# Context attentions of a Perceiver block: the third group's partial sums are joined on Pool during the last group, and the last group's weights are summed into three parts instead of six

## The chip, the cores and the metric

The kernel runs on one core of a Trainium2 chip. The core has a matrix engine (TensorE, PE in the profile, with its weight loads shown apart as PEld), three engines for elementwise work (VectorE, DVE; ScalarE, ACT; GpSimd, POOL), and SyncE (SP), whose queue issues most of the DMA transfers. Each engine works through its own list of instructions in order and waits at semaphores for the others. The metric is the device time of one execution in microseconds. Three executions of the kernel before took 1450.78, 1451.24 and 1454.07 us, median 1451.24.

## The reference: what is computed

Two layers are applied to x (512 tokens of width 512). Each has an attention to a context of 8192 rows, a self attention and a feed-forward part with 8 experts, two per token. The change touches the two context attentions alone. Cut to what matters, the first one is

```python
q = _ln(q, qn_w, qn_b) * scale
k = _ln(k, kn_w, kn_b)
attn = jnp.einsum('bihd,bjhd->bhij', q, k)
attn = jnp.where(padding_mask[:, None, None, :], attn, -jnp.inf)
p = jax.nn.softmax(attn, axis=-1)
ctx = jnp.einsum('bhij,bjhd->bihd', p, v).reshape(b, s1, c)
out = ctx @ Wo.T + bo
```

The second one has no norm of q and k and masks with -1e9 instead of -inf. Each has 16 heads of 32 columns. Of the context only the rows behind a drawn length are unmasked, at most a quarter of the 8192. The kernel looks up which tiles of 128 context rows hold unmasked rows and attends to 15 tiles (SLOTS); for more there is a second, general path, which does not run on these inputs. A softmax row is p divided by its sum, so the kernel computes unnormalised weights exp(score - max), their product with v, and their sum apart, and divides at the end.

## The kernel before, in words

Both attentions run through attend_slots (line 885). The 16 heads are taken in four groups of four (NG = 4, GH = 4), and each group passes over the 15 tiles of context rows. The main loop (line 1057) therefore has 60 steps, at = 0 to 59, with g = at // 15 the group and i = at % 15 the tile.

**One step.** PE makes four score blocks, one for each head, each 128 context rows by 512 queries, in PSUM (score, line 904, its matmul at line 905), subtracts the row maxima with a bf16 matmul (subtract, L766), and ACT takes the exponential of each block into pT, a tile of 128 x 2048 fp32 in SBUF (exp, L1055). The four heads use a quarter of the array's rows each and run side by side. accumulate (L996) multiplies pT with the values (L1010, "acc") one or two steps later. While maxima of later groups are still to be found, the steps also make a second set of scores ("scm") from which DVE takes the maxima (L934). That part is done 19 steps before the end, so the last steps have scores, shift, exponentials and acc only. Groups 0 to 2 gather acc in SBUF by DVE additions (L1018); the last group gathers it in PSUM.

**The denominators.** The sum of the weights is made by a matmul of each pT with a block of ones (denominators, L1032 to L1045, matmul at L1038, "den"). To make fewer of these, add_up (L1020) first sums up to four consecutive pT into one tile "four" (L1029). Groups 0 to 2 are summed on Pool into five parts (tiles 0 to 3, 4 to 7, 8 to 11, 12 and 13, and 14 alone). The last group is summed on DVE into six (0 to 3, 4 to 7, 8 to 11, and 12, 13 and 14 alone). For each part PE makes four matmuls, one for each head.

**The order around the change.** Work that belongs to a group already passed is put into the list fillers, and at most one entry is taken after each step. For the third group (g = 2) the entries are its denominators three steps after its end, divide one step later (ACT: Ln and Exp of d, L1044 and L1049; Pool: o x d, L1050, and + bias, L1052), and its two outputs (L855, "ops", which DVE adds into x, L861) 13 and 14 steps after its end, which is after steps i=12 and i=13 of the last group. The last group's denominators stand after its steps i=13 and i=14 and around the last two accumulations. Then finish_part (L821) makes the inverse of den, the product and the bias for one half of the queries after the other (L202, L203, L816, L819), and outputs multiplies with Wo.

**Buffers.** The scores, den and ops tiles of the last group go in turn through seven PSUM banks (tags s and m, k.tags). Tile number t in this order waits until tile t - 7 has been read: score tiles by ACT, ops tiles by DVE's addition into x. In SBUF there are five buffers for pT, five for four, one for d and two for o.

**Queues.** A scheduler of the framework orders each engine's instructions when the program is built. SP's queue at the end of the first attention loads, in this order, wva, wv, wq, two halves of wide, wo, two more of wide and a bias row; then a register load from irow (values_load in ctx_slots, L734) and the context slots (cslot, L745). wva is the value weight of the second context attention, the others belong to the self attention that comes next.

Of the kernel before, what the change touches and what calls it, by code (L numbers as in the profile page):

```python
# [11 lines left out]
F32 = mybir.dt.float32  # L12
# [5 lines left out]
ALU = mybir.AluOpType  # L18
# [3 lines left out]
P = 128  # L22
S = 512
# [6 lines left out]
NG = 4  # L30
# [35 lines left out]
def tile_perceiver(  # L66
# [5 lines left out]
    nc = tc.nc  # L72
# [127 lines left out]
    def inverse(to, src):  # L200

        nc.scalar.activation(to, src, AF.Ln)  # L202
        nc.scalar.activation(to, to, AF.Exp, scale=-1.0)  # L203
# [547 lines left out]
    def in_quads(pool, psum, pacc, qT, wo, bv, late, splits=None):  # L751
# [59 lines left out]
        def begin(g):  # L811
            k.sums[g] = [pacc.tile([P, S], F32, name=name, tag=name) for name in ("acc", "den")]

        def divided(g, r, d, acc, den):
            inverse(d[:, r], den)
            nc.vector.tensor_tensor(k.o[g][:, r], acc, d[:, r], ALU.mult)  # L816
            if bv is not None:

                nc.scalar.activation(k.o[g][:, r], k.o[g][:, r], AF.Identity, bias=bv[:, g : g + 1])  # L819

        def finish_part(g, r, acc, den):  # L821

            if g not in k.o:
                k.o[g] = late().tile([P, S], F32, name="o", tag="o", bufs=2)
            divided(g, r, late().tile([P, S], F32, name="d", tag="d", bufs=1), acc, den)

        def finish(g, pieces=1):

# [31 lines left out]
                else:  # L860
                    nc.vector.tensor_tensor(x[:, t, :], x[:, t, :], ps, ALU.add)  # L861

        k.tile_s, k.subtract, k.shift_of = tile_s, subtract, shift_of
        k.begin, k.finish, k.finish_part, k.outputs, k.quotient = begin, finish, finish_part, outputs, quotient
        return k

# [18 lines left out]
    def attend_slots(pool, psum, pacc, kT, vN, qT, kbias, krow, wo, bv, late, keys, settle, values, unit, more, early, aside, beside, extra, plan, tail, phase=None):  # L885
# [133 lines left out]

        def add_up(g, i, pT):  # L1020

            engine = nc.gpsimd if g < NG - 1 else nc.vector
            if i % 4 == 0 or i >= (n - 1 if g < NG - 1 else (n - 1) // 4 * 4):
                parts[g].append(pT)
                return
            to = parts[g][-1]
            if i % 4 == 1:
                to = late().tile([P, GH, S], F32, name="four", tag="four", bufs=5)
            engine.tensor_tensor(to, parts[g][-1], pT, ALU.add)  # L1029
            parts[g][-1] = to  # L1030

        def denominators(g, which, end):  # L1032

# [13 lines left out]
        def divide(g):  # L1047

            nc.scalar.activation(dens[g], dens[g], AF.Exp, scale=-1.0)  # L1049
            nc.gpsimd.tensor_tensor(k.o[g], k.o[g], dens[g], ALU.mult)  # L1050

            nc.gpsimd.tensor_scalar(k.o[g], k.o[g], bv[:, g : g + 1], None, ALU.add)  # L1052
# [4 lines left out]
        for at in range(NG * n):  # L1057
# [23 lines left out]
            else:  # L1081
# [6 lines left out]
                    exp(pT, h, i, tiles[h])  # L1088
                accumulate(2)
            add_up(g, i, pT)  # L1090
            if i == n - 1 and g < NG - 1:
                fillers.extend((
                    (at + 3, lambda g=g: denominators(g, range(len(parts[g])), len(parts[g]))),
                    (at + 4, lambda g=g: divide(g)),
                    (at + (13 if g == NG - 2 else 10), lambda g=g: k.outputs(g, (0, 1))),
                    (at + (14 if g == NG - 2 else 11), lambda g=g: k.outputs(g, (2, 3))),
                ))
            behind.append((g, i, pT))
            fillers.sort(key=lambda f: f[0])
            if fillers and fillers[0][0] <= at:  # L1100
                fillers.pop(0)[1]()
            if g == NG - 1 and i >= n - 2:

                lone = n - (n - 1) // 4 * 4
                whole = (n - 1) // 4
                end = whole + lone
                denominators(g, range(0, whole - 1) if i == n - 2 else range(whole - 1, end - 2), end)
        accumulate(1)
        denominators(NG - 1, range(end - 2, end), end)
        accumulate(1)  # L1110
        for _, f in fillers:
            f()
        for i in range(2):
            r = slice(i * S // 2, (i + 1) * S // 2)
            k.finish_part(NG - 1, r, k.sums[NG - 1][:, r], dens[NG - 1][:, r])
        k.outputs(NG - 1, range(NT))

    def columns(pool, vector, tag):
# [1542 lines left out]
```

## Time and profile before

| | us |
|---|---|
| median of three executions | 1451.24 |
| the profiled execution | 1449.59 |
| its span | 1447.9 |
| PE busy in it | 1408.3 |
| DVE busy | 701.3 |
| ACT busy | 582.3 |
| POOL busy | 426.7 |

The last group of the first attention runs from 345 to 394 us of the span, that of the second from 1111 to 1159 us. In lists of groups an entry is: line, engine, operation, tile written <- tiles read, shape, count, and then durations in nanoseconds as least/median/most. In timelines an entry starts with its start and its length in microseconds, and ends in brackets with the idle time before it and what ended that. In the chain of work that ended last an entry has its start, its length, the engine and the tile. fp32 matmuls have two records each, and matmuls of four heads run side by side, so 40 den records are 20 matmuls, or five parts.

### The profile page before, as it was taken

What the parts mean: (1) busy time and instruction counts of PE and PEld (TensorE: products, weight loads), DVE (VectorE), ACT (ScalarE), POOL (GpSimd) and SP (SyncE); (2) the same over time, 40 slices, a digit from 0 to 9 for tenths busy, and PEclk for the clock granted to TensorE, in tenths of its full rate; (3) what the DMA queues carried; (4) which work ended last, traced back from release to release, by engine and by line L of the source; (5) the groups of instructions that cost most, each with busy time, mean ns of one, the idle gap of its engine ahead of it and who ended that gap; (6) DMA issues with size and microseconds to landing.
All of it is one profiled execution on the core that took longest, in us unless ns stands there. A gap on an engine that the chain in (4) does not pass through costs nothing.

```text
span 1447.9 us, 25019 instructions
## 1 busy us (share of the span) xinstructions
PE 1408.3 (97%) x9827; PEld 866.4 (60%) x9827; DVE 701.3 (48%) x1987; ACT 582.3 (40%) x1168; POOL 426.7 (29%) x359
## 2 busy tenths in 40 slices
PE   8989999999999999999999999999999999999997
PEld 3434444443244558899999766644444235499993
DVE  5458598985523525111111226768986525741112
ACT  2656466677723252111111121166667822411221
POOL 2151078987011110200001110058987010111002
PEclk9999999999999999999999999999999999999999
DMA  8455200000040004987889450000000050059575
GB/s 247 152 190 148 71 31 1 2 1 1 26 185 1 15 23 164 389 304 269 270 279 302 152 178 24 30 1 2 1 1 2 1 189 1 16 207 338 192 247 183
DMA packets 94267, 175.15 MB, mean 121 GB/s; under 512 B 5496, under 2 KB 32182, under 8 KB 92348
## 3 DMA queue, kind: packets, MB, share of 16 engines
q1 hardware_dynamic: 87004, 151.43, 30.9%
q0 software_dynamic: 6416, 19.94, 3.8%
q10 hardware_dynamic: 720, 2.10, 0.4%
q8 instruction: 79, 1.29, 0.4%
q14 instruction: 48, 0.39, 0.1%
HBM read 162.72 MB, written 9.68 MB: 119 GB/s over the span
## 4 chain that ended last, share of the span: by engine, by line
PE 84%; DMA 3%; DVE 2%; ACT 1%; issue 1%; SPq 1%; POOL 0%; POOLq 0%; ACTq 0%; DVEq 0%
PE hps L2226 12%; PE y L2247 11%; PE sc L905 11%; PE acc L1010 8%; PE prj L1573 4%; PE pk L1387 4%; PE scm L923 4%; PE ops L855 3%; PE den L1038 3%; PE sc L923 3%; PE pv L1199 2%; PE sc L766 2%; DMA w<-in_L_ffn_W 2%; PE pva L1514 2%; PE pk L1199 1%; PE pv L1423 1%
## 5 line engine op out<-in xcount | busy, mean ns | idle before, releaser
L1055 ACT ACTIVATE pT<-sc,kbias 128x512 f32<-128x512 f32 x480 | 288.6, 711 | 95.6 <-PE sc L766 85.5
L934 DVE CUSTOM_DVE_ANT_0 masked<-scm,krowb 128x512 f32<-128x512 f32 (+2 forms) x400 | 213.9, 591 | 39.7 <-PE scm L923 38.1
L905 PE MATMUL sc<-qTf,kTf 32*128 32x512 f32 x960 | 216.7, 621 | 1.5 <-DVE tops L934 1.5
L2226 PE MATMUL hps<-tokens,w 128*128 128x160 f32 (+11 forms) x1408 | 194.3, 294 | 3.5 <-DMA w<-in_L_ffn_W 3.5
L2226 PEld LDWEIGHTS hps<-tokens,w 128*128 128x128 f32 x1408 | 185.5, 192 | 6.5 <-issue 3.8
L923 PE MATMUL scm<-kTf,qTf 32*128 32x512 f32 (+2 forms) x800 | 189.0, 539 | 0.0
L2247 PE MATMUL y<-hT,w 128*128 128x160 f32 (+11 forms) x1280 | 177.2, 297 | 1.1 <-DMA w<-in_L_ffn_W 1.1
L2247 PEld LDWEIGHTS y<-hT,w 128*128 128x128 f32 x1280 | 170.1, 192 | 3.6 <-DVE hT L2480 1.1
L1029 POOL TENSOR_TENSOR four<-four,pT 128x2048 f32<-128x2048 f32 x36 | 164.0, 4555 | 1.6
L905 PEld LDWEIGHTS sc<-qTf,kTf 32*128 32x128 f32 x960 | 73.7, 183 | 95.6 <-DVE tops L934 42.5
L1010 PE MATMUL acc<-pT,vNf 128*32 128x512 f32 x960 | 127.8, 604 | 0.0
L1029 POOL TENSOR_TENSOR four<-pT 128x2048 f32<-128x2048 f32 x24 | 109.3, 4556 | 54.0 <-ACT pT L1055 54.0
L934 DVE CUSTOM_DVE_ANT_0 masked<-sc,krowb 128x512 f32<-128x512 f32 (+2 forms) x176 | 98.5, 614 | 54.9 <-PE sc L923 54.5
L2475 DVE TENSOR_TENSOR hT<-sg,hps 128x264 f32<-128x264 f32 (+7 forms) x64 | 28.0, 437 | 194.5 <-ACT sg L2474 187.6
L2474 ACT ACTIVATE sg<-hps 128x264 f32<-128x264 f32 (+7 forms) x64 | 25.4, 397 | 180.1 <-PE hps L2226 175.3
L923 PEld LDWEIGHTS scm<-kTf,qTf 32*128 32x128 f32 x800 | 86.1, 184 | 15.3 <-issue 6.2
L766 PE MATMUL sc<-shift,ones 3*128 3x512 bf16 (+3 forms) x544 | 93.4, 367 | 0.0
L2278 POOL DMA_DIRECT2D answers_d<-yb x17 | 9.6, 566 | 243.4 <-ACT yb L2265 243.2
L1018 DVE TENSOR_TENSOR o<-o,acc 128x512 f32<-128x512 f32 x84 | 57.4, 683 | 20.5 <-PE acc L1010 20.5
L1010 PEld LDWEIGHTS acc<-pT,vNf 128*32 128x32 f32 x960 | 19.3, 108 | 70.3 <-DVE tops L934 34.7
L1199 PE MATMUL pv<-wkvf,cslot 128*128 128x512 f32 x120 | 54.9, 606 | 1.8 <-DVE tops L934 1.1
L1656 DVE TENSOR_REDUCE neg<-sc 128x1 f32<-128x512 f32 (+3 forms) x64 | 26.9, 484 | 60.0 <-PE sc L1652 60.0
(394 smaller groups left out, 1874.0 us busy)
## 6 DMA issues: line engine op xcount, KB each, us to landing
w<-in_L_ffn_W SPq DMA_DIRECT2D x94, 1024.0 KB, 5.4
mi<-in_mask SPq DMA_DIRECT2D x32, 512.0 KB, 4.6
cslot<-in_ctxT SPq DMA_DIRECT2D x40, 256.0 KB, 3.9
answers_d<-yb POOLq DMA_DIRECT2D x13, 256.0 KB, 4.0
answers_d<-zero POOLq DMA_DIRECT2D x9, 256.0 KB, 3.0
wkvf<-in_L_xattn_WkvT SPq DMA_DIRECT2D x8, 256.0 KB, 6.9
wof<-in_L_xattn_WoT SPq DMA_DIRECT2D x2, 1024.0 KB
wide<-in_L_attn_wk SPq DMA_DIRECT2D x4, 512.0 KB
```

The costliest lines, as they stand in the source:

```text
L766: nc.tensor.matmul(ps, lhsT=ones16[r, :], rhs=k.shifts[g][r, 0:w], start=start, stop=stop)
L905: nc.tensor.matmul(ps, lhsT=kT[HD * h : HD * (h + 1), g, i * P : (i + 1) * P], rhs=qT[HD * h : HD * (h + 1), g, :], start=True, stop=stop,)
L923: nc.tensor.matmul(ps[:, at : at + w], lhsT=qT[HD * h : HD * (h + 1), g, t * P : (t + 1) * P], rhs=kT[HD * h : HD * (h + 1), g, lo : lo + ...
L934: nc.vector.tensor_tensor_reduce(masked[:, 0:w], ps[:, at : at + w], krow[:, lo : lo + w], 1.0, -BIG, ALU.add, ALU.max, accum_out=tops[g % ...
L1010: nc.tensor.matmul(acc[HD * h : HD * (h + 1), :], lhsT=vN[:, i, g * P + HD * h : g * P + HD * (h + 1)], rhs=pT[:, h, :], start=alone or i ...
L1029: engine.tensor_tensor(to, parts[g][-1], pT, ALU.add)
L1055: nc.scalar.activation(pT[:, h, :], ps, AF.Exp, bias=kbias[:, i : i + 1])
L1199: last = nc.tensor.matmul(ps.rearrange("p (g n) -> p g n", g=NG), lhsT=src[:, c, s % 2, :], rhs=wkv[:, :, c, i * P : (i + 1) * P], start=( ...
L1387: end = nc.tensor.matmul(ps[:, j], lhsT=wk[:, g, c], rhs=src[:, c], start=(c == 0), stop=(c == NC - 1))
L1573: nc.tensor.matmul(ps, lhsT=w(c), rhs=xnT[:, c, off : off + S], start=(c == 0), stop=(c == NC - 1))
L2226: end = nc.tensor.matmul(ps[:, j, 0:k], lhsT=w1[:, c, f * P : (f + 1) * P], rhs=tokens[:, c, starts[r] : starts[r] + k], start=(c == 0), s ...
L2247: nc.tensor.matmul(accs[0][:, d, 0:k], lhsT=w2[:, f, d * P : (d + 1) * P], rhs=hT[:, f, 0:k], start=(c == 0 and f == 0 and d % 2 == 0), st ...
```

## The change

For the third group, three additions are put on Pool after step i=14 (fewer): the part of tile 14 into that of tiles 12 and 13, and the parts of tiles 0 to 3 and 4 to 7 into that of tiles 8 to 11. Two parts stay instead of five. Its denominators come eight steps after the group's end instead of three, divide nine instead of four; the outputs stay where they were.

For the last group, tile 12 is added to the part of tiles 8 to 11 on DVE; the part of tiles 0 to 3 is added to that of 4 to 7 on Pool at step i=8, and the result to that of 8 to 11 on DVE at step i=11. Three parts stay instead of six: tiles 0 to 12, 13 and 14. Their matmuls stand after the loop, with no den matmuls after steps i=13 and i=14.

At the end, the inverses of both halves are made before both products, in one tile d for both.

In the built program the order of PE, DVE, ACT and POOL differs from before in these places only. On DVE the new join and the addition of tile 12 stand ahead of the four additions of the third group's ops into x. On ACT the last Ln, Ln, Exp, Exp, + bias, + bias replace Ln, Exp, + bias twice. On SP the register load from irow and the first cslot load now stand between wva and wv at the end of the first attention; the second attention's order on SP is as before.

```diff
--- before.py
+++ after.py
@@ -811,9 +811,8 @@
         def begin(g):
             k.sums[g] = [pacc.tile([P, S], F32, name=name, tag=name) for name in ("acc", "den")]
 
-        def divided(g, r, d, acc, den):
-            inverse(d[:, r], den)
-            nc.vector.tensor_tensor(k.o[g][:, r], acc, d[:, r], ALU.mult)
+        def divided(g, r, d, acc):
+            nc.vector.tensor_tensor(k.o[g][:, r], acc, d, ALU.mult)
             if bv is not None:
 
                 nc.scalar.activation(k.o[g][:, r], k.o[g][:, r], AF.Identity, bias=bv[:, g : g + 1])
@@ -822,7 +821,9 @@
 
             if g not in k.o:
                 k.o[g] = late().tile([P, S], F32, name="o", tag="o", bufs=2)
-            divided(g, r, late().tile([P, S], F32, name="d", tag="d", bufs=1), acc, den)
+            d = late().tile([P, S], F32, name="d", tag="d", bufs=1)
+            inverse(d[:, r], den)
+            divided(g, r, d[:, r], acc)
 
         def finish(g, pieces=1):
 
@@ -860,7 +861,7 @@
                 else:
                     nc.vector.tensor_tensor(x[:, t, :], x[:, t, :], ps, ALU.add)
 
-        k.tile_s, k.subtract, k.shift_of = tile_s, subtract, shift_of
+        k.tile_s, k.subtract, k.shift_of, k.divided = tile_s, subtract, shift_of, divided
         k.begin, k.finish, k.finish_part, k.outputs, k.quotient = begin, finish, finish_part, outputs, quotient
         return k
 
@@ -1019,15 +1020,28 @@
 
         def add_up(g, i, pT):
 
-            engine = nc.gpsimd if g < NG - 1 else nc.vector
-            if i % 4 == 0 or i >= (n - 1 if g < NG - 1 else (n - 1) // 4 * 4):
+            final = g == NG - 1
+            if i % 4 == 0 and not (final and i >= n - 3) or i >= n - (2 if final else 1):
                 parts[g].append(pT)
                 return
             to = parts[g][-1]
             if i % 4 == 1:
                 to = late().tile([P, GH, S], F32, name="four", tag="four", bufs=5)
-            engine.tensor_tensor(to, parts[g][-1], pT, ALU.add)
+            (nc.vector if final else nc.gpsimd).tensor_tensor(to, parts[g][-1], pT, ALU.add)
             parts[g][-1] = to
+            if final and i == n - 4:
+                join(g, 1, 0, nc.vector)
+
+        def join(g, to, of, engine):
+
+            pin(engine.tensor_tensor(parts[g][to], parts[g][to], parts[g][of], ALU.add))
+            parts[g].pop(of)
+
+        def fewer(g):
+
+            join(g, 3, 4, nc.gpsimd)
+            join(g, 1, 0, nc.gpsimd)
+            join(g, 1, 0, nc.gpsimd)
 
         def denominators(g, which, end):
 
@@ -1088,10 +1102,13 @@
                     exp(pT, h, i, tiles[h])
                 accumulate(2)
             add_up(g, i, pT)
+            if i == n - 1 and g == NG - 2:
+                fewer(g)
             if i == n - 1 and g < NG - 1:
+                rest = 8 if g == NG - 2 else 3
                 fillers.extend((
-                    (at + 3, lambda g=g: denominators(g, range(len(parts[g])), len(parts[g]))),
-                    (at + 4, lambda g=g: divide(g)),
+                    (at + rest, lambda g=g: denominators(g, range(len(parts[g])), len(parts[g]))),
+                    (at + rest + 1, lambda g=g: divide(g)),
                     (at + (13 if g == NG - 2 else 10), lambda g=g: k.outputs(g, (0, 1))),
                     (at + (14 if g == NG - 2 else 11), lambda g=g: k.outputs(g, (2, 3))),
                 ))
@@ -1099,20 +1116,22 @@
             fillers.sort(key=lambda f: f[0])
             if fillers and fillers[0][0] <= at:
                 fillers.pop(0)[1]()
-            if g == NG - 1 and i >= n - 2:
-
-                lone = n - (n - 1) // 4 * 4
-                whole = (n - 1) // 4
-                end = whole + lone
-                denominators(g, range(0, whole - 1) if i == n - 2 else range(whole - 1, end - 2), end)
+            if g == NG - 1 and i == n // 2 + 1:
+                join(g, 1, 0, nc.gpsimd)
+        end = len(parts[NG - 1])
+        denominators(NG - 1, (0,), end)
         accumulate(1)
-        denominators(NG - 1, range(end - 2, end), end)
+        denominators(NG - 1, range(1, end), end)
         accumulate(1)
         for _, f in fillers:
             f()
+        r = slice(0, S // 2), slice(S // 2, S)
+        d = late().tile([P, S], F32, name="d", tag="d", bufs=1)
+        k.o[NG - 1] = late().tile([P, S], F32, name="o", tag="o", bufs=2)
         for i in range(2):
-            r = slice(i * S // 2, (i + 1) * S // 2)
-            k.finish_part(NG - 1, r, k.sums[NG - 1][:, r], dens[NG - 1][:, r])
+            inverse(d[:, r[i]], dens[NG - 1][:, r[i]])
+        for i in range(2):
+            k.divided(NG - 1, r[i], d[:, r[i]], k.sums[NG - 1][:, r[i]])
         k.outputs(NG - 1, range(NT))
 
     def columns(pool, vector, tag):
```

## The prediction

> **What bounds the kernel now.** I read the page first. TensorE (PE) is busy for 97% of the span, so the change can pay only by taking work off PE, and only where PE does not then wait for the engine that took the work over.
>
> ```profile
> PE 1408.3 (97%) x9827; PEld 866.4 (60%) x9827; DVE 701.3 (48%) x1987; ACT 582.3 (40%) x1168; POOL 426.7 (29%) x359
> ```
>
> Next the chain of work that ended last, in the last group of the first attention (335 to 400 us):
>
> ```profile
> 351.80 4.29 PE den L1038 x40
> 356.09 1.07 PE sc L905 x8
> 357.17 0.22 PE sc L766 x4
> 357.38 0.99 PE acc L1010 x8
> ...
> 378.99 1.91 PE ops L855 x4
> ...
> 383.19 1.91 PE ops L855 x4
> 385.10 1.85 PE den L1038 x16
> ...
> 389.24 1.72 PE den L1038 x16
> ...
> 391.81 1.84 PE den L1038 x16
> ...
> 394.89 6.80 DMA wv<-in_L_attn_wv
> ```
>
> It is PE without a break. One step (scores, shift, acc) is 1.07 + 0.22 + 0.99 = 2.28 us; 40 den records, that is five parts, are 4.29, so a part is 0.86 us. ACT needs 0.58 for each of a step's four exponentials, 2.33 us, hardly more than PE's step.
>
> Last the adds that the change gives to Pool and DVE, by line 1029 and by the timelines of both engines:
>
> ```profile
> L1029 POOL TENSOR_TENSOR four<-four,pT x36: 4536/4554/4572, 191.8 to 1105.9; 128x2048 f32<-128x2048 f32 x36
> L1029 DVE TENSOR_TENSOR four<-four,pT x12: 2291/2293/2294, 353.6 to 1144.3; 128x2048 f32<-128x2048 f32 x12
> ```
> ```profile
> 344.78 4.56 POOL L1029 TENSOR_TENSOR four<-pT 128x2048 f32<-128x2048 f32 x1
> ```
> ```profile
> 351.16 2.29 DVE L1029 TENSOR_TENSOR four<-pT 128x2048 f32<-128x2048 f32 x1 [0.88 <-ACT pT L1055]
> ```
>
> In this kernel Pool's last add ends (349.34) before DVE's first begins (351.16): the two never add side by side. After the change they do. What happens then shows elsewhere: a 64x15 DVE instruction that ends with a Pool add, and small and large Pool instructions that begin while DVE reads two SBUF operands.
>
> ```profile
> 205.59 4.55 POOL L1029 TENSOR_TENSOR four<-four,pT 128x2048 f32<-128x2048 f32 x1
> ```
> ```profile
> 207.78 2.38 DVE L694 TENSOR_SCALAR taken<-steps,place,some 64x15 f32<-64x15 f32 x1
> ```
> ```profile
> L694 DVE TENSOR_SCALAR taken<-steps,place,some x2: 285/1334/2383, 6.3 to 207.8; 64x15 f32<-64x15 f32 x2
> ```
> ```profile
> 120.24 0.69 DVE L1354 TENSOR_TENSOR kb<-kb,un_v 128x512 f32<-128x512 f32 x1
> ```
> ```profile
> L1464 POOL TENSOR_SCALAR first<-mi x32: 207/218/762, 34.2 to 172.0; 128x2 f32<-128x2 int32 x32
> ```
>
> The 64x15 instruction takes 0.285 us alone and 2.383 here: it ends at 210.16, the Pool add at 210.14. In the other direction a Pool instruction of 0.218 us, begun at 120.25, takes 0.762 and ends at 121.01, just after the DVE add at 120.93. So each engine waits for the other's whole instruction, up to a handover: Pool lets go about 0.285 - 0.02 = 0.26 us before its end, DVE about 0.218 - 0.08 = 0.14.
>
> **The change, part by part.** Per attention (there are two):
>
> Off PE: the third group's den has two parts for five, the last group's three for six; 6 x 0.86 = 5.1 us off the path.
>
> Onto Pool: three joins of 4.55 us behind its last add of the third group, and one more at step i=8 of the last group. In Pool's queue o x d and + bias (1.28 and 1.57 us) stand behind the first three, the fourth behind these. Onto DVE: one join and the add of i=12, 2.29 us each; behind them in its queue stand the four adds into x that empty the PSUM banks of ops. On PE the moved den waits for the third join, on ACT the two activations on d wait for that den, and the exponentials of i=8 on stand behind them.
>
> Without any contest for the port I replayed the last group, each engine in its order, each instruction at its row's duration when engine and inputs are ready, 0.1 us for a semaphore. The same replay of before ends at 394.39, the trace's last acc at 394.35. Pool's joins run from 349.37 to 363.11. PE, no longer held by den at 351.80, comes to den after five steps at 363.24, just behind them. DVE then does i=11 to 378.1, the join to 380.5, i=12 from 380.6 to 382.9, and only then the first add into x, to 383.7. PE wants the bank that this empties at 381.5, for the second ops of i=13, and gets it at 383.8: 2.3 us lost. The last acc ends at 391.34, so 3.05 us earlier per attention.
>
> With the port as those rows show it, the two alternate. Join 1: 349.37 to 353.92. DVE's add of i=1, ready at 351.08, gets the port at 353.66 and ends at 355.96; join 2 355.82 to 360.37; add 2 to 362.41; join 3 362.27 to 366.82. PE's den starts at 366.92 for 363.24: 3.7 us lost. DVE goes on late: add 3 to 368.85, add 5 to 371.25, then behind o x d add 6 to 374.42, behind + bias add 7 to 377.88, add 9 to 380.28. The fourth join takes 380.14 to 384.69; adds 10 and 11 end at 389.12, the join on DVE at 391.51, i=12 at 393.90, the first add into x at 394.69. PE would have made that second ops at 385.22 and makes it at 394.79: 9.6 us lost. The last acc ends at 402.33 for 394.39, 7.9 us later; so -5.1 + 3.7 + 9.6, and some small change.
>
> The unknown price is the handover. Held to the very end of each instruction, the replay gives +10.2 us; let go by Pool 0.9 before its end and by DVE 0.14, +4.1; if Pool keeps the port from join 1 into join 2 (no wait stands between them), +8.5. I take +7.9, by the two rows, and keep +3.5 to +10.4.
>
> The Trainium skill (SBUF — State Buffer, section SBUF: two separate sides) states that a DVE instruction with two SBUF inputs and a Pool instruction that reads SBUF lock each other out for the full instruction, which speaks against this change. By the rule alone it would be +10.2. One row differs from it: a DVE add that starts at 359.86 while Pool's + bias lasts from 358.88 to 360.45, and neither is longer than elsewhere; so the rows' handover goes before the rule.
>
> The tail. Both Ln now stand before the first Exp on ACT, so the first half of o comes one Ln (0.38 us) later, and ops, norm and the next stage with it: +0.4. The second half comes earlier, hidden under the two ops of the first half (1.9 us). On SP the first attention's order changes: a register load from irow and one cslot load (256 KB) come between wva and wv. The register load's rows are 1.4 to 1.6 us and the issue 0.4, so wv is issued 2 us later. That lies under wva's own transfer (1 MB, some 2.4 us at the 430 GB/s of that stretch); cslot's 256 KB take 0.6 us in front of wv. PE waits for wv there already (1.5 us), so between 0 and 2.6 us; I take +0.7, which covers the 0.4 of this attention too. The second attention's SP order is the same.
>
> At nothing: the freed buffers. The weights of i=14 are freed by join 1 (353.92), before the exponentials of i=4 want them (355.6); the sums' buffers by joins 2 and 3, before adds 5 and 9. If Pool came 2 us later still, these would wait first.
>
> Sum: 2 x 7.9 + 0.7 + 0.4 = +16.9 us. The profiled execution took 1449.59 us (span 1447.9), so 1466.5; it lies 1.65 under the median 1451.24, and for the median I say 1468.
>
> **The rivals.** First, no contest between the two adds (the faster side). For it: the row at 359.86, with 0.59 us of overlap and no delay. Against: the 2.1 us wait at 207.78, though of an instruction of another kind. It gives 2 x -3.05 + 1.1 = -5.0, 1446. The point from which it decides: DVE's i=12 ends at 382.9 there, and every us that this comes later moves the end by about as much; one block of 2.5 us per attention eats it.
>
> Second, only Pool waits: DVE takes the port at once. For it: Pool's 0.762 at 120.25, and a Pool add of 4.93 us at 72.60 beside 4.52 elsewhere. Against: 207.78 again. Joins then end at 364.9, den waits 1.8 us, the fourth join ends at 375.6; -1.4 per attention, with the tail -1.7: 1449.5, no change.
>
> Third, Pool keeps the port over all its joins. For it: Pool's adds follow each other within 0.05 us. Against: the 64x15 instruction did get in between two Pool adds. It gives +9.0 per attention: 1470.
>
> **How the numbers follow.** Alternation, with the third rival as its upper end, 85%; only Pool waits 8%; no contest 7%. A measurement of this kernel tells about 0.3%, 4.4 us, from no change: no contest at -5.0 stands at the edge and gives faster 6% and same 1%; only Pool waits is same; alternation at +3.5 to +10.4 per attention, +8 to +22, is all slower. The likeliest one's own range is 1459 to 1474. The range leaves out the two rivals below, and reaches a little past the handovers on both sides: 1456 to 1476.
>
> **What would show it.** In the changed profile: DVE's adds of line 1029's group longer than 2.29 us, or starting well after their exponentials, beside Pool's joins, up to 4 us each; PE's den of the third group waiting some 3 to 4 us for Pool; PE's second ops of i=13 waiting some 9 us for DVE's add into x; the last group, 49.4 us from its first scores (344.95) to its last acc, about 57. Den records 240 where there were 336. The prediction is wrong if DVE's adds stay at 2.29 us and follow their exponentials at once: then the port is not contested. It is wrong in size if PE's two waits are there but the joins end well before 366.

## The result, and the profile after

The changed kernel took 1472.43 us, the median of four executions (1469.55 to 1473.89); the kernel before took 1451.01 beside it (1449.29 to 1454.07). The ratio is 1.0143, with a 95% interval from 1.0119 to 1.0166: 21.4 us slower. The forecast was 1468 with a range of 1456 to 1476. The profiled execution took 1473.18 us, its span 1471.5 (before: 1447.9).

First the page's line of busy time:

```profile
PE 1410.4 (96%) x9731; PEld 863.8 (59%) x9731; DVE 745.6 (51%) x1991; ACT 581.5 (40%) x1168; POOL 480.9 (33%) x367
```

PE has 96 records fewer, the den that the change took off it, and is nevertheless busy for 2.1 us more: some of its instructions must have become longer. The chain of work that ended last, in the last group of the first attention, is no longer PE without a break (start, length, what):

```profile
349.64 11.07 POOL four L1037 x2
...
360.79 6.46 POOL four L1037
...
367.29 3.69 PE den L1052 x16
...
372.34 2.79 POOL o L1064
...
375.21 3.48 POOL o L1066
378.69 5.95 POOL four L1037
...
405.56 1.39 SPq L734
...
407.59 5.84 DMA wv<-in_L_attn_wv
```

Pool's joins (L1037) stand where PE's scores and accumulations stood; the second and third take 6.5 us each instead of the 4.5 of such an add. The same stretch on DVE, as a timeline (start, length, line; in brackets the idle time before):

```profile
351.40 4.92 DVE L1030 TENSOR_TENSOR four<-pT 128x2048 f32<-128x2048 f32 x1 [0.88 <-ACT pT L1069]
356.42 12.96 DVE L1030 TENSOR_TENSOR four<-four,pT 128x2048 f32<-128x2048 f32 x2
...
380.35 8.84 DVE L1030 TENSOR_TENSOR four<-four,pT 128x2048 f32<-128x2048 f32 x2
389.29 2.29 DVE L1037 TENSOR_TENSOR four<-four 128x2048 f32<-128x2048 f32 x1
391.69 2.29 DVE L1030 TENSOR_TENSOR four<-four,pT 128x2048 f32<-128x2048 f32 x1
393.89 1.88 DVE L862 TENSOR_TENSOR x<-x,ops 128x512 f32<-128x512 f32 x3
```

The first three adds take 4.92 and 12.96 us where three times 2.29 would do, as long as Pool's joins last; two more take 8.84 beside the fourth join. The first add into x can only begin at 393.89. And on PE:

```profile
367.29 3.64 PE L1052 MATMUL den<-four,ones 128*32 128x512 f32 x16 [3.31 <-POOL four L1037]
370.86 2.03 PE L906 MATMUL sc<-qTf,kTf 32*128 32x512 f32 x8
...
394.63 2.08 PE L856 MATMUL ops<-wof,o 128*128 128x512 f32 x2 [6.14 <-DVE x L862]
396.64 2.09 PE L906 MATMUL sc<-qTf,kTf 32*128 32x512 f32 x8
```

These are the two waits that were forecast: 3.3 us for Pool's third join and 6.1 us for DVE's first add into x. Not forecast is what follows each of them: 16 den records take 3.64 us, eight score records 2.03 and 2.09. In the same view of before they take 1.92 and 1.14:

```profile
385.03 1.92 PE L1038 MATMUL den<-four,ones 128*32 128x512 f32 x16
386.88 1.14 PE L905 MATMUL sc<-qTf,kTf 32*128 32x512 f32 x8
```

The windows of the profile after say why (stretch, its length, busy time and count of the five engines, then PE's granted clock):

```profile
366.00:372.60 6.60, 5.31 (x24) 1.28 (x28) 6.50 (x3) 1.23 (x2) 1.50 (x2) 0.50 0.00 0
372.90:393.00 20.10, 15.60 (x118) 4.04 (x114) 18.89 (x7) 14.08 (x24) 11.64 (x3) 1.00 0.00 1
393.40:399.80 6.40, 5.17 (x18) 1.39 (x22) 3.06 (x5) 0.57 (x1) 0.00 (x0) 0.50 0.00 0
400.10:405.00 4.90, 4.90 (x49) 1.28 (x39) 0.00 (x0) 2.32 (x6) 0.02 (x1) 1.00 0.01 2
```

PE's clock is at half for some 6.5 us around the end of each wait. In before it is whole all through the last group.

Two lengths, read from the PE timelines, carry the comparison from here on: the last group (from its first scores to the end of its last acc) and the tail (from there to the first projection of the next stage, vps). Attention 1 / 2, in us:

| profile | last group | tail |
|---|---|---|
| before, three executions | 49.5 / 49.5 each | 7.4 to 7.6 / 9.0 |
| after | 59.7 / 58.3 | 8.7 / 9.6 |
| after, once more | 58.2 / 60.2 | 8.7 / 9.1 |
| third group's part alone | 53.7 / 52.6 | 7.6 / 9.4 |
| last group's part and new end | 53.2 / 54.4 | 8.5 / 9.1 |
| the same with Pool memsets | 54.3 / 55.7 | 8.4 / 9.1 |
| new end alone | 49.5 / 49.5 | 8.5 / 9.6 |
| PE kept at work in its waits | 56.8 / 56.9 | 8.8 / 9.2 |
| adds into x first on DVE | 54.5 / 54.0 | 8.9 / 9.1 |
| all joins on DVE, two executions | 46.4 / 46.4 each | 7.5, 7.6 / 9.0 |

### The profile page after: what moved, and what is told of

It reads as the page before. It is cut to its first block, busy times and chain, and to the rows that moved or that the text cites. A ratio compares the mean times of both kernels' runs of the same rounds, so it can differ in the third digit from the quotient of the medians.

```text
span 1471.5 us, 24845 instructions
## 1 busy us (share of the span) xinstructions
PE 1410.4 (96%) x9731; PEld 863.8 (59%) x9731; DVE 745.6 (51%) x1991; ACT 581.5 (40%) x1168; POOL 480.9 (33%) x367
## 4 chain that ended last, share of the span: by engine, by line
PE 79%; DVE 5%; issue 3%; POOL 2%; DMA 2%; ACT 1%; SPq 1%; DVEq 0%; POOLq 0%; ACTq 0%
PE hps L2245 11%; PE y L2266 11%; PE sc L906 9%; PE acc L1011 6%; PE prj L1592 4%; PE pk L1406 4%; PE scm L924 4%; PE ops L856 3%; PE sc L924 3%; PE pv L1218 3%; DVE four L1030 2%; PE pva L1533 2%; PE sc L766 2%; PE den L1052 2%; POOL four L1037 2%
## 5 line engine op out<-in xcount | busy, mean ns | idle before, releaser
L906 PE MATMUL sc<-qTf,kTf 32*128 32x512 f32 x960 | 220.1, 632 | 1.5 <-DVE tops L935 1.5
L1030 DVE TENSOR_TENSOR four<-four,pT 128x2048 f32<-128x2048 f32 x14 | 58.9, 4209 | 1.5
```

Of the source, the lines that this page charges most:

```text
L906: nc.tensor.matmul(ps, lhsT=kT[HD * h : HD * (h + 1), g, i * P : (i + 1) * P], rhs=qT[HD * h : HD * (h + 1), g, :], start=True, stop=stop,)
L1030: (nc.vector if final else nc.gpsimd).tensor_tensor(to, parts[g][-1], pT, ALU.add)
```

## The experiments

Theory A is that of the prediction: Pool's joins and DVE's adds lock each other out of SBUF, instruction by instruction, and PE pays twice, at the den that waits for the third join and at the bank that DVE's first add into x frees. Theory B is the first rival, no contest.

**The parts one by one.** `e1_third_only` has the third group's joins and its later den in the kernel before; the last group and the end are those of before.

```diff
+            if i == n - 1 and g == NG - 2:
+                fewer(g)
             if i == n - 1 and g < NG - 1:
+                rest = 8 if g == NG - 2 else 3
...
-                    (at + 3, lambda g=g: denominators(g, range(len(parts[g])), len(parts[g]))),
-                    (at + 4, lambda g=g: divide(g)),
+                    (at + rest, lambda g=g: denominators(g, range(len(parts[g])), len(parts[g]))),
+                    (at + rest + 1, lambda g=g: divide(g)),
```

> The third group's part of the change alone: its three joins on Pool, its den of two parts eight steps after its end. The last group (six parts) and the end are as before. Theory A (a Pool add and a DVE add hold each other up for a whole instruction, and PE's clock halves for some us behind each long wait of PE): Pool's second and third join and DVE's adds of steps 1 to 3 last longer than 4.55 and 2.29 us, PE's den waits about 3.5 us for the third join, and each attention ends about 3 us later than before in the replay, so about 1457 us. Theory B (no contest for the port; the loss of the change comes from the order of DVE's queue and from the end): the joins last 4.55 us, den does not wait, and 2.6 us are saved per attention, so about 1446.

It took 1457.39 us against 1452.35 of before, ratio 1.0032 (1.0013 to 1.0050). Its timelines of DVE and of PE:

```profile
351.15 4.93 DVE L1029 TENSOR_TENSOR four<-pT 128x2048 f32<-128x2048 f32 x1 [0.88 <-ACT pT L1066]
356.18 12.97 DVE L1029 TENSOR_TENSOR four<-four,pT 128x2048 f32<-128x2048 f32 x2
```
```profile
367.06 3.64 PE L1049 MATMUL den<-four,ones 128*32 128x512 f32 x16 [3.33 <-POOL four L1034]
```

The adds are held up and the den waits as in the changed kernel. DVE's first add into x, with no join and no add of i=12 ahead of it, comes at 384.89, and PE does not wait for it.

`e2_last_only` is the other half: the last group's new sums and the new end, with the third group's den in five parts and at its old place.

```diff
-            if i == n - 1 and g == NG - 2:
-                fewer(g)
             if i == n - 1 and g < NG - 1:
-                rest = 8 if g == NG - 2 else 3
+                rest = 3
```

(against the changed kernel)

> The last group's part alone: three parts, one join on Pool and one on DVE, tile 12 added on DVE, and the new order at the end. The third group is as before (five parts, no joins). Theory A: DVE's add beside the one Pool join lasts until it is done, the adds into x come behind that, PE's second ops of step 13 waits some 6 us; +3.7 us per attention in the replay and +1.1 for the end, so about 1459. Theory B: only the order of DVE's queue costs, 2.3 us of wait, which the three parts saved just pay for: about 1451.

It took 1461.65 us, ratio 1.0069 (1.0042 to 1.0096). Its timelines, one line of DVE, one of Pool and one of PE:

```profile
373.90 4.69 DVE L1030 TENSOR_TENSOR four<-pT 128x2048 f32<-128x2048 f32 x1 [2.15 <-ACT pT L1069]
```
```profile
371.90 4.54 POOL L1037 TENSOR_TENSOR four<-four 128x2048 f32<-128x2048 f32 x1 [11.34 <-DVE four L1030]
```
```profile
388.82 1.69 PE L856 MATMUL ops<-wof,o 128*128 128x512 f32 x2 [4.48 <-DVE x L862]
```

The one join begins at 371.90 and ends at 376.44; DVE's add, on record from 373.90, ends at 378.59, so its 2.29 us of work began at 376.3. A single Pool add thus costs DVE 2.4 us, and with the join and the add of i=12 ahead of the adds into x, PE waits 4.5 us. Both parts lose by themselves; the lengths of the last group grow by 4.2 and 3.7 us in attention 1.

**What Pool does to DVE.** `e3_memsets` puts six Pool memsets in the place of the three joins. It leaves the sums of tiles 0 to 7 and of tile 14 out of the third group's denominators.

```diff
-            join(g, 3, 4, nc.gpsimd)
-            join(g, 1, 0, nc.gpsimd)
-            join(g, 1, 0, nc.gpsimd)
+            for of in (0, 0, 0, 0, 1, 1):
+                pin(nc.gpsimd.memset(parts[g][of], 0.0))
+            del parts[g][4], parts[g][0], parts[g][0]
```

> The changed kernel, with the third group's three joins replaced by six memsets on Pool into the tiles of the parts that are dropped, so Pool is about as busy in that stretch but reads no SBUF; the sums of tiles 0 to 7 and 14 are left out of the third group's denominators. The fourth join stays. Theory A (it is the reading of SBUF that holds DVE up): DVE's adds of steps 1 to 3 are back at 2.29 us, den does not wait, and what is left of the loss is that of the fourth join: about 1457. If any Pool instruction beside DVE's adds holds them up: adds longer than 2.29 us, and the time stays near 1472.

The whole took 7797 us, a number of no use: from 1648 us on the general path runs (8192 matmul records of L432, of which before has none), and why it does was not followed up. The last group of the first attention lies ahead of that, and there Pool's and DVE's timelines do answer the question:

```profile
352.67 11.02 POOL L1043 MEMSET four<- 128x2048 f32 x6
```
```profile
354.57 2.29 DVE L1030 TENSOR_TENSOR four<-pT 128x2048 f32<-128x2048 f32 x1 [0.88 <-POOL four L1043]
356.96 4.69 DVE L1030 TENSOR_TENSOR four<-four,pT 128x2048 f32<-128x2048 f32 x2
```

DVE's adds are back at 2.29 us each beside 11 us of memsets, and PE's den, at 366.96, does not wait. For a time that can be compared there is `f4_unread`, which computes all that before computes: e2_last_only with sixty Pool memsets of a tile that nobody reads.

```diff
         def fewer(g):
-            join(g, 3, 4, nc.gpsimd)
-            join(g, 1, 0, nc.gpsimd)
-            join(g, 1, 0, nc.gpsimd)
+            junk = late().tile([P, 128], F32, name="junk", tag="junk", bufs=1)
+            for _ in range(60):
+                pin(nc.gpsimd.memset(junk, 0.0))
...
+            if i == n - 1 and g == NG - 2:
+                fewer(g)
```

> The kernel before with the last group's part of the change and the new end (the run e2_last_only, 1461.7 us), and sixty Pool memsets of 128x128 into a tile that nobody reads, put where the changed kernel has its three joins: Pool is busy for some 12 us beside DVE's adds of i=1 to 3, and reads no SBUF. Theory A (it is Pool's reading of SBUF that holds DVE's adds up, not Pool's being busy): those adds last 2.29 us each, and the time is that of e2_last_only, 1461 to 1463. Rival B (any Pool instruction takes the port for its length): DVE's adds come some 6 to 10 us later, PE's second ops of i=13 waits for that, and the time is 1466 to 1475.

It took 1463.0 us against 1451.73, ratio 1.0073 (1.0055 to 1.0091); e2_last_only has 1.0069. Pool's and DVE's timelines:

```profile
350.90 15.73 POOL L1044 MEMSET junk<- 128x128 f32 x60
```
```profile
352.79 2.29 DVE L1030 TENSOR_TENSOR four<-pT 128x2048 f32<-128x2048 f32 x1 [0.88 <-POOL junk L1044]
355.19 2.29 DVE L1030 TENSOR_TENSOR four<-four,pT 128x2048 f32<-128x2048 f32 x1
361.49 2.29 DVE L1030 TENSOR_TENSOR four<-four,pT 128x2048 f32<-128x2048 f32 x1 [4.01 <-ACT pT L1069]
```

For 15.7 us Pool is at work, writing only, and DVE's adds stay at 2.29 us; none of the memsets is longer than 0.22 us either. So what holds DVE's adds up is not that Pool is at work, nor that it writes: the joins read SBUF, the memsets do not. (PE's second ops waits 5.7 us here for 4.5 in e2_last_only: Pool's o x d and + bias stand behind the memsets, at 366.59 and 369.72, and DVE's adds of that time run into them.) (The "<-POOL junk" in brackets is the profile's guess of a releaser; the add follows its exponential by the usual 0.88 us.) The Trainium skill (SBUF — State Buffer, section Who interferes with whom) says just this, and the rows agree: a DVE instruction with two SBUF inputs is in the way of a GpSimd instruction that reads SBUF, not of one that only writes it.

**The place in DVE's queue.** `f2_x_first` is the changed kernel with DVE's last join and its add of i=12 behind the first two adds into x.

```diff
-            if i % 4 == 0 and not (final and i >= n - 3) or i >= n - (2 if final else 1):
+            if i % 4 == 0 or i >= n - (2 if final else 1):
...
-            if final and i == n - 4:
-                join(g, 1, 0, nc.vector)
...
+            if g == NG - 1 and i == n - 3:
+                join(g, 1, 0, nc.vector)
+                join(g, 0, 1, nc.vector)
```

> The changed kernel (1472.4 us), with DVE's last join and its add of i=12 put behind the first two adds into x instead of ahead of them. Work and engines are the same. Theory A (PE's long wait is for the place in DVE's queue as well as for DVE's delay): DVE's first add into x comes 4.6 us earlier, at about 390, PE's wait for it falls from 6.1 to about 1.5 to 2 us, the last acc comes 4.2 us earlier per attention: 1464 (1462 to 1466). Rival B (what counts is how late DVE is with all its adds, wherever the adds into x stand, since the last den waits for i=12): 1471 to 1473.

It took 1461.37 us, ratio 1.0071 (1.0049 to 1.0093), 11 us less than the changed kernel and 2.6 less than expected. DVE's and PE's timelines:

```profile
387.75 1.28 DVE L862 TENSOR_TENSOR x<-x,ops 128x512 f32<-128x512 f32 x2
388.94 2.29 DVE L1035 TENSOR_TENSOR four<-four 128x2048 f32<-128x2048 f32 x1
```
```profile
388.48 1.12 PE L856 MATMUL ops<-wof,o 128*128 128x512 f32 x2 [1.35 <-DVE x L862]
389.54 1.14 PE L906 MATMUL sc<-qTf,kTf 32*128 32x512 f32 x8
...
393.77 1.07 PE L1050 MATMUL den<-four,ones 128*32 128x512 f32 x8 [1.88 <-DVE four L1035]
```

The wait for the add into x falls from 6.1 to 1.35 us; in exchange the last den now waits 1.9 us for the add of i=12. It is better than expected, and PE's lengths say where: after the short wait ops and scores run at full speed (1.12 and 1.14 us instead of 2.08 and 2.09). In the second attention, after a wait of 1.89 us, the ops do too (1.13), but the scores behind them take 1.64 us; there the granted clock is 0.50 from 1159.8 to 1163.1 us.

**The clock.** `f1_warm` is the changed kernel with matmuls that nobody needs in PE's two waits, so that PE never stands idle there; each wait still ends when Pool and DVE are done. (The ten of the second wait went into the bank of the first of the two ops, which the ops then overwrites.)

```diff
                     dens[g] = tile_s(name="den")
+                    if g == NG - 2:
+                        for i in range(16):
+                            h = i % GH
+                            pin(nc.tensor.matmul(
+                                dens[g][HD * h : HD * (h + 1), :], lhsT=k.ones32, rhs=vN[:, 0, :], start=True, stop=True
+                            ))
...
+            if g == NG - 2 and tuple(tiles) == (2, 3) and k.warm is not None:
+                for _ in range(10):
+                    pin(nc.tensor.matmul(both[0][1], lhsT=ident, rhs=k.warm, start=True, stop=True))
```

> The changed kernel (1472.4 us), with matmuls that are not needed put on PE in its two waits of each attention: four rounds (3.4 us) into the den tile ahead of the third group's den, ten 128x512 matmuls (8.6 us) into the PSUM bank of the second ops of i=13, whose results the matmuls that follow overwrite. Nothing else moves. Theory C (PE's clock halves after its waits, and that is what the prediction left out): the third group's den lasts 1.7 us again for 3.6, the scores after the second ops 1.0 to 1.1 for 2.1, the granted clock of the stretch 345 to 405 us is 1.00 for 0.89; DVE's first add into x, which releases the second ops, stays at 394.7; the last acc starts at about 402 for 404.3; so 2.3 to 2.5 us less per attention, and up to 2.5 more where layer 1's wait at vps lowers the clock as well: 1465 to 1468. Rival D (the clock is not what lengthens those matmuls; PE shares something with the engines that add): the matmuls stay as long as they are, the time stays at 1472, or rises to 1476 where the added matmuls outlast the waits.

It took 1466.26 us, ratio 1.0096 (1.0078 to 1.0114): with more work on PE it is 6 us faster than the changed kernel. PE's timeline and the window of the stretch:

```profile
366.53 1.92 PE L1062 MATMUL den<-four,ones 128*32 128x512 f32 x16
368.38 1.14 PE L910 MATMUL sc<-qTf,kTf 32*128 32x512 f32 x8
...
384.00 8.85 PE L854 MATMUL ops<-vNf,ident 128*128 128x512 f32 x20
392.69 1.88 PE L859 MATMUL ops<-wof,o 128*128 128x512 f32 x4
```
```profile
345.00:405.00 60.00, 59.70 (x423) 18.01 (x413) 47.36 (x23) 39.73 (x72) 33.90 (x9) 1.00 0.05 16
```

The den is back to 1.92 us, the scores to 1.14, and the granted clock is 1.00 throughout, while the joins end at the same place (third join at 366.47, in a group that began 0.8 us earlier). The last group is 56.8 us long. So the halved clock lengthens the last group by what the changed kernel has above that, 1.4 to 3.4 us. Nearly all of it comes behind the second wait. From the group's first scores to the second ops it takes 49.0 to 49.8 us in the two profiles of the changed kernel and 49.3 here; from there to the end of the last acc 9.3 to 10.4 us against 7.6. The slow matmuls behind the first wait only bring PE later to the second one, whose end DVE sets.

**The end.** `f3_end_only` is the kernel before with the new end alone, and with it the new order on SP.

```diff
+        r = slice(0, S // 2), slice(S // 2, S)
+        d = late().tile([P, S], F32, name="d", tag="d", bufs=1)
+        k.o[NG - 1] = late().tile([P, S], F32, name="o", tag="o", bufs=2)
         for i in range(2):
-            r = slice(i * S // 2, (i + 1) * S // 2)
-            k.finish_part(NG - 1, r, k.sums[NG - 1][:, r], dens[NG - 1][:, r])
+            inverse(d[:, r[i]], dens[NG - 1][:, r[i]])
+        for i in range(2):
+            k.divided(NG - 1, r[i], d[:, r[i]], k.sums[NG - 1][:, r[i]])
```

> The kernel before (1451.2 us) with the new end alone: the inverses of both halves (Ln, Ln, Exp, Exp on ACT) ahead of both products, and SP's order at the end of the first attention as in the changed kernel (a register load and a cslot load between wva and wv). Theory A (the tail's two terms, +0.7 and +0.4): 1452.3, at most 1454, with PE's wait for wv 0 to 1.2 us longer than the 1.5 of before. Rival B (the tail is free, wv lies under wva's transfer): 1451.0 to 1451.5.

It took 1453.06 us against 1451.73, ratio 1.0006 (0.9996 to 1.0017). The time alone cannot tell +1.1 from nothing; the profile can. In PE's timeline

```profile
404.82 1.95 PE L1621 MATMUL vps<-wv,xnT 128*128 128x512 f32 x4 [2.50 <-DMA wv<-in_L_attn_wv]
```

the wait for wv is 2.5 us (1.5 to 1.7 in before), and the tails are 1.0 and 0.6 us longer, with the last group at its old 49.5. Most of the 0.6 is the clock: here and in the first profile of the changed kernel (9.6 us each) it falls some 2 us before the end of that tail, as it does in e1_third_only, which has the old end and 9.4; in the five other profiles with this end it falls less than 1 us before or later, and the tail has 9.1 to 9.2, that is 0.1 to 0.2 more than before.

**Without Pool.** `e4_dve` keeps the aim, fewer den matmuls, but has no join on Pool: one join of the third group (four parts, den six steps after the group's end) and three additions of the last group run on DVE, the last two of them behind the first two adds into x; the end is the old one.

```diff
+            if g == NG - 1 and i == 1:
+                join(g - 1, 3, 4, nc.vector)
             add_up(g, i, pT)
...
-            if i == n - 1 and g == NG - 2:
-                fewer(g)
...
-                rest = 8 if g == NG - 2 else 3
+                rest = 6 if g == NG - 2 else 3
...
-            if g == NG - 1 and i == n // 2 + 1:
-                join(g, 1, 0, nc.gpsimd)
+            if g == NG - 1 and i == n // 2:
+                join(g, 1, 0, nc.vector)
+            if g == NG - 1 and i == n - 3:
+                join(g, 1, 0, nc.vector)
+                join(g, 0, 1, nc.vector)
```

(against the changed kernel)

> No joins on Pool. DVE makes the join of tile 14 into the part of tiles 12 and 13 of the third group before its own first add (four parts instead of five, den six steps after the group's end), the join of tiles 0 to 3 into 4 to 7 at step 7, and, behind the first two adds into x, the join into 8 to 11 and the add of tile 12 (three parts). The end is as before. Theory A: no add of either engine is held up but by Pool's product and bias, no long wait of PE, and four parts (3.4 us) come off PE per attention; 3.1 to 3.6 us in the replay, so about 1444 to 1445. If DVE has no room for these adds, PE's ops or last den waits and the time is at 1451 or above.

It took 1444.19 us against 1452.35, ratio 0.9942 (0.9919 to 0.9964), and beats both kernels. DVE's and PE's timelines:

```profile
379.59 1.28 DVE L862 TENSOR_TENSOR x<-x,ops 128x512 f32<-128x512 f32 x2
380.79 2.29 DVE L1035 TENSOR_TENSOR four<-four 128x2048 f32<-128x2048 f32 x1
383.18 2.29 DVE L1035 TENSOR_TENSOR four<-four,pT 128x2048 f32<-128x2048 f32 x1
```
```profile
382.00 1.98 PE L856 MATMUL ops<-wof,o 128*128 128x512 f32 x4
```

No add is longer than 2.29 us, PE does not wait at its second ops, and the last group is 3.1 us shorter than before in both attentions: four den parts fewer by 0.86 us are 3.4. A second look at the same kernel:

> The run e4_dve (all joins on DVE, 1444.2 us) once more, for one more profile. Its PE has no wait over 2 us inside the last group, so theory and rival of the clock both say: first exponential to last acc 208.6 us in the first attention (211.8 before), 1441 to 1446.

It took 1443.9 us; the last group was 46.4 us again in both attentions, and from the first exponential to the last acc it was 208.7 in the first.

**Profiles repeated.** One figure did not fit. In layer 1 PE waits 2.9 us ahead of its projections (vps) in every kernel. From the first to the last of these it took 18.3 us in the profile of before and 20.8 in that of after, though the change touches nothing there. Three profiles were taken anew, of before twice and of the changed kernel once.

> The kernel before once more, for one more profile. Open point: in layer 1 PE waits 2.9 us for a DVE result ahead of its value projections (vps) in all kernels; behind this wait the clock stayed whole in the first profile of before (first to last vps 18.3 us) and fell to half in that of the changed kernel (20.8 us). Theory E (whether the clock falls after a wait of this length depends on when in a fixed period of the chip the wait comes, so it differs between executions of one program): this stretch takes another length than 18.3 in at least one of the two repeated profiles of before, or another than 20.8 in that of the changed kernel. Rival F (it belongs to the program): 18.3 in each profile of before, 20.8 of the changed kernel. Time 1447 to 1455 either way.

> The kernel before a third time, for the same question. Theory E: the vps stretch of layer 1 takes between 18.3 and 20.8 us, not the same in all three profiles. Rival F: 18.3 again.

> The changed kernel once more, for one more profile. Theory E: PE's clock is at half behind its two long waits in each attention (3.3 and 6 to 7 us) as in the first profile, the third group's den 3 to 3.7 us long, while the vps stretch of layer 1 takes 18.3 to 20.8 us. Rival F: 20.8 again. Both: 1469 to 1475, and the last acc of the first attention 221 to 223 us behind the first exponential.

They took 1454.02, 1454.24 and 1475.34 us, one execution each (before beside them: 1448.95). The stretch took 20.0 us in both of before, and 19.9 in the changed kernel. PE's timeline in the first profile of before and in the third (the transposes lnt alternate with vps):

```profile
1167.87 0.66 PE L287 MATMUL lnt<-ident,xn_all 128*128 128x128 f32 x4 [2.87 <-DVE overs L2526]
1170.82 0.60 PE L287 MATMUL lnt<-ident,xn_all 128*128 128x128 f32 x4
```
```profile
1170.58 0.66 PE L287 MATMUL lnt<-ident,xn_all 128*128 128x128 f32 x4 [2.87 <-DVE overs L2526]
1174.66 1.06 PE L287 MATMUL lnt<-ident,xn_all 128*128 128x128 f32 x4
```

The same wait, 2.87 us, in the same program: in one execution the next lnt comes 2.95 us later and is short, in the other 4.08 us later and long. So the 2.5 us there are not the change's, but belong to the execution; rival F falls. In the repeated profile of the changed kernel the two waits of each attention lower the clock again (den 3.28 and 3.64 us, ops 2.08 and 2.07). One part of its expectation failed: from the first exponential to the last acc the first attention took 224.1 us, not 221 to 223. Its last group explains none of it (58.2 us against 59.7); it lost its time earlier, where the window from 200 to 220 us has a granted clock of 0.84 and 220 to 240 one of 0.91, while the first profile has 1.00 from 182 to 345.

## Why the prediction was right, and where it fell short

**The mechanism: right, and closely.** The last group began 0.25 us later than in before's profile. The third join ended at 367.25 (forecast 366.82), DVE's add of i=12 at 393.98 (393.90), PE's second ops of i=13 began at 394.63 (394.79). The alternation is in the joins' 6.5 us, an add of each engine, 4.54 + 2.29 = 6.83, less some 0.3 of handover. The prediction had preferred its rows (0.26 and 0.14 us of handover) to the rule of a lock for the full instruction, and the runs are on that side. PE's waits are at the two places that were named, 3.3 us where 3.7 was forecast and 6.1 where 9.6 was; the second is short because of the clock, as follows.

**The rivals.** No contest and only Pool waits are ruled out by DVE's adds of 4.92 and 6.5 us. Pool keeps the port is ruled out by the first of them: it ends at 356.32, in the midst of the second and third join (354.12 to 367.23).

**The size: the term that failed is the one of the last group, +7.9 us per attention.** Measured are +10.2 and +8.8, and in the repeated profile +8.7 and +10.7, a mean of 9.6. The replay priced each wait by its own length and let PE go on at full clock afterwards. The runs put in its place: around each of these waits, of 3.3 us or more, the clock is at half for 3.4 or 6.8 us, and the matmuls behind the wait are slow. With PE kept at work (f1_warm) the term is 7.3 us in both attentions, 0.6 below the forecast; there the matmuls that nobody needs hold PE for 3.4 us at the first place and, to the start of the second ops, 8.7 at the second. So the waits were sized nearly right, 0.6 us too high together, and the clock's 1.4 to 3.4 us per attention were missing. In the changed kernel the second wait is 6.1 us and not 8.7 because the slow den and scores behind the first have used up the difference. Before's profile had a mark of it, which the prediction did not use: from 395 to 405 us, around the wait for wv, the granted clock is 0.86.

The Trainium skill (TensorE: Matmul & The Clock Gate, section What's actually happening) states that an idle window of about 3.4 us halves PE's clock, that about as much busy time restores it, and that these windows run freely. The record of the clock in the profiles agrees with the length and the free running: leaving e3_memsets out, all stretches of half clock in a profile begin on one grid of 3.413 us, to within 3 ns, and last 3.41 or 6.83 us (once 10.24), but for the one that the program's end cuts off. It does not agree that a whole window must be idle: waits of 3.31 us are shorter than one, and all eight of that length lowered the clock. The page also puts the cost of the ramp at under 1% of a typical span; here what the clock costs in the two attentions, 2 x (9.6 - 7.3) = 4.6 us, is 0.3% of the span, but a fifth of the whole difference.

**The tail: undersized in the first attention.** +0.7 for the first attention measured +1.2: the register load and the cslot load put wv's issue at 407.59, 2.7 us behind the last acc (394.89, 0.5 behind it, in before), and PE's wait for wv grew from 1.5 to 2.6. The range given, 0 to 2.6, held. +0.4 for the second measured +0.6, most of it the clock, and +0.15 in the repeated profile, where the clock falls only 0.2 us before that tail's end; that term was too high.

**The sum.** Two profiles of the changed kernel give 2 x 9.6 for the last groups and 1.6 for the tails, 20.8 of the 21.4 us between the medians. The forecast's 16.9 lacked 3.4 of the first (4.6 for the clock, less 1.2 by which the waits were put too high) and 0.5 of the second, some of it the clock as well. The difference between the two spans first profiled, 23.6 us, holds another 2.5 that are the chance of the layer 1 wait.

**What a part of the change is worth.** The two parts lose 4.2 and 3.7 us in the first attention by themselves, 7.9 together, and 10.2 when combined (9.6 in the mean of the four last groups). DVE's first add into x shows why. Counted from the group's first scores, it comes 4.1 us later than in before with the first part, 7.2 with the second and 12.8 with both; alone, the 4.1 us cost nothing at that place, since PE does not wait there, and behind the longer queue they do.

## What to carry to other kernels

Before work is moved from the bound engine to Pool and DVE together, look whether DVE's instructions have two SBUF operands while Pool's read SBUF: the two are then one resource, and their durations add (here 6.5 us for adds of 4.54 and 2.29). In front of an instruction that the bound engine waits for (here the add that frees a PSUM bank), put nothing in the queue that could stand behind it; that alone, with the clock that came with it, was worth 11 of the 21 us here. And a wait of PE of some 2 us or more can cost 1 to 3 us beyond its length, for the slow clock behind it, unless a later wait hides that; so do not read a difference of 1 to 3 us out of one pair of profiles where PE has such waits.

## What was not expected of the hardware

- PE's granted clock halves after its waits. All eight den waits of 3.31 to 3.34 us in the profiles here (after, after once more, e1_third_only, f2_x_first; two attentions each) were followed by den records 3.28 to 3.64 us long instead of 1.92, and all eight ops waits of 4.5 to 6.8 us (after, after once more, e2_last_only, f4_unread) by ops of 1.69 to 2.08 us instead of 1.12. After ops waits of 1.35 and 1.89 us (f2_x_first) they were 1.12 and 1.13, but behind the 1.89 us the clock fell all the same, 1.6 us later.
- Between these lengths it differs from execution to execution of one program: 2.87 us left the clock whole in one of three profiles of before, and lowered it in two. The profiles show most of what this hangs on: how the wait lies on the grid of 3.413 us. The wait that left the clock whole (1164.99 to 1167.87) is cut by the grid at 1166.78 into 1.79 and 1.09 us; a wait of 3.54 us in f1_warm (602.52 to 606.06), cut at 604.30 into 1.78 and 1.76, left it whole too; the 1.89 us in f2_x_first lie almost wholly in the slot from 1156.35 to 1159.76, and at its end the clock fell. From 110 us on, 45 slots began at full clock and had PE busy for less than 47.5%: 42 of them ended with the lowered clock, and one of the 50 with 47.5 to 62%. It is not the whole rule: 15 more falls, at 504 to 523 and 1266 to 1299 us, follow slots with a busier PE and are not explained.
- Pool's memsets, 15.7 us of small ones in f4_unread and 11.0 us of large ones in e3_memsets, cost DVE's adds of two SBUF operands nothing, while one Pool add of 4.54 us cost them 2.4.
